# Turning softmax weights with VectorE block transposes and a round trip through DRAM instead of TensorE transposes

## The chip, the core and the metric

The kernel runs on one core of a Trainium2 chip. A core has five instruction streams that each run in order: TensorE (PE, matrix products, with its weight loads shown apart as PEld), VectorE (DVE), ScalarE (ACT), GpSimd (POOL) and SyncE (SP), which here issues nearly all DMA transfers. The metric is the device time of one execution in microseconds (us). Before the change it is 1191.92 us, the median of three runs (1191.44 to 1193.4).

## The reference, cut to what matters

Four transformer layers run one after the other over 8 batch entries of 128 tokens by 256 features, all in float32. Every layer attends to the same context of 8 x 128 x 256 (`ctx`) in some way and ends in a feed-forward network of 1024 hidden units. The first two layers have 16 heads of 16 features and turn no weights in this kernel. What the change touches is the attention of the third and the fourth layer:

```python
# third layer, twice (i = 1, 2): 16 heads of K = 128 features, one learned key and value more
qh = (q_in @ wq + bq).reshape(b, q_len, H, K)
kh = concat([(kv_in @ wk + bk).reshape(b, t, H, K), bias_k])
vh = concat([(kv_in @ wv + bv).reshape(b, t, H, K), bias_v])
logits = einsum('bqhk,bthk->bhqt', qh, kh) / sqrt(K)
weights = softmax(logits)                       # over t
ctx = einsum('bhqt,bthk->bqhk', weights, vh).reshape(b, q_len, H * K)
x = res + ctx @ wo + bo

# fourth layer: self attention (w_qkv), then attention to ctx (w_q, w_kv); 16 heads of 16
scores = einsum('bhqd,bhkd->bhqk', q, k) / sqrt(16)
scores = scores * mask - 10000.0 * (1.0 - mask)
probs = softmax(scores)
out = einsum('bhqk,bhkd->bhqd', probs, v)
```

In both, the scores come out with the queries on the 128 partitions and the keys along the row, so that the softmax is taken along a row. The second product sums over the keys, and TensorE sums over partitions: so the 128 x 128 weights of every head have to be turned (keys onto the partitions) between the softmax and that product.

## The kernel before

**Tiling.** The batch is cut into four threads of two entries each (`SIZES`, class `Thread`, lines 483 to 499). A thread goes through all four layers (`blocks`, line 1434): the first two in `front` (1464), the third as two calls of `wide_attention` (1223) and an `mlp`, the fourth in `last_block` (1489) as attentions "a4" and "a5" and an `mlp`. Threads are in different layers at the same time: a thread starts its front when the thread two before it has left its own (`FRONTS`), and at most three are ahead of the end of the third layer (`WIDES`). The last thread (number 3) does its fourth layer entry by entry (`BY_BATCH`).

**Third layer.** `wide_attention` goes over four groups of four heads (`group`, 1301). A group makes keys, queries and values of both entries, and then for each entry the scores of four heads into one PSUM bank ("tl", tile `s`) and `after_scores` (1374): the maximum (`mx`), the difference into tile `t` (128 x 516: four heads of 128 keys and the learned key at the end of each head's row), the exponential in place, the row sums (`sm`), their reciprocal, and the scaling on POOL. Then four TensorE transposes (`transposes`, 1394) take `t` against the identity `ident` into another "tl" bank; `out_of` (1204) copies it to SBUF (`pt`) on ACT or DVE, whichever is asked first; four products with the values `vw` (`weighted`, 1403) follow, and the output projection. This is done 4 threads x 2 attentions x 4 groups x 2 entries = 64 times. A `t` buffer (7 of them) is free after the transposes, a `pt` buffer (`pt_wide`, 2) after `weighted`.

**Fourth layer.** `attention` calls `by_pairs` (1103). For an entry, 16 heads' scores fill four PSUM banks ("sc"); `softmax` (1128) handles one bank of four heads (index r): scores times mask (DVE), plus the mask's second term (POOL), minimum (`mn`, DVE; signs are flipped), four exponentials with their sums (ACT), reciprocal (DVE), scaling (POOL). `values` (1152) then turns the four tiles `ts[r]` one after the other by four TensorE transposes each, copies each out (`out_of`) to its part of `pts`, and runs 32 small products (`weighted`). That is 4 threads x 2 attentions x 2 entries x 4 = 64 tiles more.

**The value bias of the third layer.** The learned value is taken out of the values: `value_bias` (1361) loads 512 numbers of `L2_bv` and 512 of `L2_bias_v` to all partitions (tiles `bv`, 2 buffers, and `bb`, 1 buffer; 256 KB each), subtracts the second from the first on POOL, and does so for every group of every thread, 32 times. `learned_keys` (1215) does the like for the keys once.

**What sets the order.** All instructions are written out once by a planner (class `Plan`, 85). Each piece of work is a Python generator with an urgency (smaller is sooner); the planner keeps a clock with a modelled duration per instruction (`_weight`, 265), and whenever an engine of the model is free, it emits on that engine the ready piece with the smallest urgency. Urgencies are the table `U` (66) plus an offset per thread and stage from `LATE` (67). Every buffer is a `Slots` counter. So the order on each engine, SP's too, is fixed at build time; on the chip an instruction waits for its inputs and holds up all that is behind it on its engine. DMA transfers go through `load` and `dma` (437 to 450), which the planner holds for done when its modelled transfer is over:

```python
        plan.dma_until = max(plan.dma_until, plan.now) + kb_ * 2.75
        yield plan.dma_until - plan.now + 2300
```

When TensorE has nothing to do and the model finds its clock in danger, `idle_work` (422) emits a product of the identity with itself. Almost every instruction passes through one helper, so that the profile puts it on line 335; the tiles' names tell them apart. A float32 product is two MATMUL records in the profile, a transpose one.

Of the kernel before, what the change touches and what calls it, by code (L numbers as in the profile page):

```python
# [14 lines left out]
AF = mybir.ActivationFunctionType  # L15
ALU = mybir.AluOpType
AX = mybir.AxisListType

P = 128
# [41 lines left out]

WARM = True
FRONTS, WIDES = 2, 3
FRONT_BY_BATCH, BY_BATCH = (0,), (3,)
AHEAD = [[(1, 0), (1, 1)], [], [], []]
U = {'take': 0.75, 'taken': -1, 'norm': 1.9, 'mask': 5.29, 'k': 2.24, 'q': 0.77, 'v': 3.01, 'by key': 0.17, 'softmax': 1.71, 'weights': 1.17, 'pairs': 0.21, 'out': 0.57, 'mlp norm': -0.61, 'mlp 1': 2.92, 'mlp 2': 3.24, 'wide norm': -0.65, 'wide k': 3.4, 'wide q': 3.13, 'wide v': 6.35, 'wide s': 4.05, 'wide': 0.91, 'ahead': 3.88, 'load': -0.56, 'early': 2.38}
LATE = [(3.86, -0.62, -1, 1.19, 0.57, -0.78, 2.63, 2.91, 2.96, 4.12, 2.25, 1.84, 0.96, 5.29, 0.08, 0.08, 1.89), (2.66, 9.69, 3.46, 1.89, 2.36, 5.53, 5.25, 5.05, 6.11, 13.74, 3.59, 9.93, 12.52, 6.5, 10.81, 5.73, 5.27), (4.81, 10.83, 3.75, -1, -0.06, 1.37, 3.1, 2.75, 1.5, 1.56, 0.96, -1, -1, 8.35, 14.37, 7.29, 0.32), (1.56, 2.87, 0.11, -0.46, 1.42, 1.31, 4.51, 3.52, 0.3, -0.41, -1, 3.2, -0.53, 2.26, 3.5700000000000003, 0.86, 0.98)]


class Event:  # L70
# [194 lines left out]
def _weight(eng, name, args, kw):  # L265
# [25 lines left out]
    if eng == "DVE":  # L291
        if name == "tensor_scalar" and n == 4 and len(aps) == 2 and len(args) > 5:
            return 145, False
        if name == "reciprocal":
            return 65 + 6.25 * n, False
        if name in ("bn_stats", "bn_aggr"):
            return (330 if name == "bn_stats" else 150), False
        if n <= 8:
            return 68 + 55 * max(0, len(aps) - 2) * (name == "tensor_scalar"), on_sbuf and name != "memset"
        if name in ("tensor_scalar", "tensor_copy") and on_sbuf:  # L300
            return 75 + 0.8 * n + 55 * by_part, True
        two = name in ("tensor_tensor", "scalar_tensor_tensor") and sum(
            x.space == bass.MemoryType.SB and x.free_size() > 1 for x in aps[1:]) == 2
        return 72 + 1.03 * n + 55 * by_part, two
# [52 lines left out]
def four_blocks(ctx: ExitStack, tc: tile.TileContext, a: dict, out: bass.AP):  # L357
# [2 lines left out]
    wpool = ctx.enter_context(tc.tile_pool(name="w", bufs=1))  # L360
    act = ctx.enter_context(tc.tile_pool(name="act", bufs=1))
    ps = ctx.enter_context(tc.tile_pool(name="ps", bufs=1, space=bass.MemoryType.PSUM))
    plan = Plan()
    nc = Engines(tc.nc, plan)
    spawn = plan.spawn
# [20 lines left out]
        return t[:, : n * w].rearrange("p (a b) -> p a b", a=n)  # L386


    NT_, NHT, NXN, NAT = 7, 4, 2, 2
    t_slots, hT_slots, xn_slots, at_slots = Slots(NT_), Slots(NHT), Slots(NXN), Slots(NAT)  # L390
    pt_small, pt_wide, tm_slots = Slots(2), Slots(2), Slots(2)
    kb_slots, v_slots = Slots(20), Slots(4)
    attn_slots, x1_slots = Slots(4), Slots(4)
    row_slots, bv_slots, bb_slots, w_slots = Slots(2), Slots(2), Slots(1), Slots(NWT)

    def kb():
        return new(act, [P, 2 * P], "kb", bufs=20)
# [705 lines left out]
    def by_pairs(T, ns, scale, mask, masks, q, k, v, v_in, vb, attnT):  # L1103
# [24 lines left out]
        def softmax(s, b, r, mn, sm, ts):  # L1128
            s = s.rearrange("p (h k) -> p h k", h=4)
            yield (t_slots, 1)  # L1130
            t = ts[r] = new(act, [P, 516], "t", bufs=NT_)[:, :512].rearrange("p (h k) -> p h k", h=4)
            bm = b % masks

            def over_heads(i):
                return mask[:, i, bm, :].unsqueeze(1).to_broadcast([P, 4, P])
            yield op("DVE", lambda: nc.vector.tensor_tensor(t, s, over_heads(0), ALU.mult))
            plan.put(sc)
            yield op("POOL", lambda: nc.gpsimd.tensor_tensor(t, t, over_heads(1), ALU.add))
            yield op("DVE", lambda: nc.vector.tensor_reduce(mn[:, r].unsqueeze(2), t, AX.X, ALU.min))

            def exps():
                for j in range(4):
                    nc.scalar.activation(
                        t[:, j, :], t[:, j, :], AF.Exp, bias=mn[:, r, j : j + 1], scale=-1.0,
                        accum_out=sm[:, r, j],
                    )
            yield op("ACT", exps, None, EXP)
            yield op("DVE", lambda: nc.vector.reciprocal(sm[:, r], sm[:, r]))
            yield op("POOL", lambda: nc.gpsimd.tensor_tensor(
                t, t, sm[:, r].to_broadcast([P, 4, P]), ALU.mult))  # L1150

        def values(b, soft, ts, turn, next_turn):
            yield turn
            pts, evs = None, []
            for r in range(4):
                yield soft[r]
                if r == 0:
                    yield (pt_small, 1)
                    pts = new(act, [P, 4, 4, P], "pt4", bufs=2)
                yield (tl, 1)  # L1160
                pt = parts(bank("tl"), 4, P)

                def transposes():
                    for i in range(4):
                        nc.tensor.transpose(
                            pt[:, i, :], ts[r].rearrange("p h k -> p (h k)")[:, i * P : (i + 1) * P], ident
                        )
                yield op("PE", transposes, 0)
                plan.put(t_slots)
                evs.append(spawn(out_of(pt, pts[:, r]), U["weights"] + late, Plan.SEEN["PE"]))  # L1170
# [6 lines left out]
            def weighted():  # L1177
                for i, (c, e) in enumerate(heads):
                    for r in range(4):
                        nc.tensor.matmul(  # L1180
                            av[32 * r : 32 * r + 32, c, :],
                            lhsT=v[:, 0, b, 4 * c + r, 16 * e : 16 * e + 32],
                            rhs=pts[:, r, i, :], start=(e == 0), stop=(e == 1),
                        )
            yield op("PE", weighted)
            plan.put(pt_small)
# [24 lines left out]

    kbs = {}
    kbs_in = Event()

    def learned_keys():
        yield cols_in
        for i in (1, 2):
            kbs[i] = new(const, [P, 16], f"kb{i}")
            yield op("POOL", lambda: nc.gpsimd.tensor_tensor(
                kbs[i], col(f"L2_bk{i}", 0, 16), col(f"L2_bias_k{i}", 0, 16), ALU.subtract))  # L1220
        plan.set(kbs_in)

    def wide_attention(T, i):
        hT, hT_in = yield from normed(
# [136 lines left out]
    def value_bias(to, i, hg, step_back):  # L1361
# [1 line left out]
        yield (bv_slots, 1)  # L1363
        bv = new(wpool, [P, 512], "bv", bufs=2)
        to.append(bv)
        e = spawn(load(bv, a[f"L2_bv{i}"][:, s].partition_broadcast(P), 256), U["load"] + step_back)
        yield (bb_slots, 1)
        bb = new(wpool, [P, 512], "bb", bufs=1)
        yield spawn(load(bb, a[f"L2_bias_v{i}"][:, s].partition_broadcast(P), 256), U["load"] + step_back)
        yield e  # L1370
        yield op("POOL", lambda: nc.gpsimd.tensor_tensor(bv, bv, bb, ALU.subtract))
        plan.put(bb_slots)

    def after_scores(T, i, hg, b, s, vs, v_in, n, v_slots):
        t = new(act, [P, 516], "t", bufs=NT_).rearrange("p (h k) -> p h k", h=4)
        mx = new(act, [P, 4, 1], "mx", bufs=4)
        sm = new(act, [P, 4, 1], "sm2", bufs=4)
        yield op("DVE", lambda: nc.vector.tensor_reduce(mx, s, AX.X, ALU.max))
        yield op("DVE", lambda: nc.vector.tensor_scalar(t[:, :, P : P + 1], mx, 0.0, -1.0, ALU.max, ALU.mult))
        yield op("DVE", lambda: nc.vector.tensor_tensor(  # L1380
            t[:, :, 0:P], s, t[:, :, P : P + 1].to_broadcast([P, 4, P]), ALU.add))
        plan.put(tl)
        yield op("ACT", lambda: nc.scalar.activation(t, t, AF.Exp), None, EXP)
        yield op("DVE", lambda: nc.vector.tensor_reduce(sm, t, AX.X, ALU.add))
        yield op("DVE", lambda: nc.vector.reciprocal(sm, sm))
        yield op("POOL", lambda: nc.gpsimd.tensor_tensor(
            t[:, :, 0:P], t[:, :, 0:P], sm.to_broadcast([P, 4, P]), ALU.mult))
        yield v_in
        yield (pt_wide, 1)
        yield (tl, 1)  # L1390
        pt = parts(bank("tl"), 4, P)
        dst = new(act, [P, 4, P], "pt", bufs=2)

        def transposes():
            for j in range(4):
                nc.tensor.transpose(pt[:, j, :], t[:, j, 0:P], ident)
        yield op("PE", transposes)
        plan.put(t_slots)
        yield from out_of(pt, dst)
        yield (tl, 1)  # L1400
        av = parts(bank("tl"), 4, P)

        def weighted():
            for j in range(4):
                nc.tensor.matmul(
                    av[:, j, :], lhsT=vs[b][:, j * P : (j + 1) * P], rhs=dst[:, j, :], start=True, stop=True)
        yield op("PE", weighted)
        plan.put(pt_wide)
        plan.put(v_slots)
# [112 lines left out]
    plan.idle_work = idle_work if WARM else None  # L1522
    spawn(inputs(), 0)
    spawn(learned_keys(), 5.0)
    plan.run()


# [40 lines left out]
```

## Time and profile before

| | |
|---|---|
| runs | 1191.44, 1191.92, 1193.4 us (median 1191.92) |
| profiled execution: span from the first to the last instruction | 1188.3 us |
| PE busy | 1151.0 us |
| DVE, ACT, POOL busy | 747.5, 595.0, 345.3 us |
| DMA | 146.61 MB, 39.3% of the engines' span in the main queue |
| transposes of the weights | 512, in quartets of one tile `t` |
| granted TensorE clock | 0.997 |

The profile is of one execution. The page gives no other time of it than its span; the median of the timed runs is 3.6 us longer. Busy time of an engine is the union of its instructions. In the groups of instructions, `out<-in` are tile names without numbers, then the shapes, then busy time, mean ns of one, and the idle time of the engine just before. A matmul's mean duration (some 275 ns for the smallest) is its passage through the pipeline; several overlap, so the time that one takes from TensorE is read from the starts in the timeline. The DMA list gives the size of a transfer and the median time from issue to landing.

### The profile page before, as it was taken

How to read it: one execution, taken by the hardware profiler on the slowest of the kernel's cores; microseconds unless marked ns; L12 is line 12 of the kernel's file. 1: busy time of each engine (PE TensorE's matmuls, PEld its weight loads, DVE VectorE, ACT ScalarE, POOL GpSimd, SP SyncE). 2: the span in 40 equal slices, each digit the busy share in tenths (PEclk: the TensorE clock that was granted, in tenths of full speed). 3: DMA queues.
4: the chain of work that ended last, by engine and by line, in shares of the span. 5: the costliest groups of instructions: out<-in, count | busy, mean ns of one | idle time of the engine just before them, and what ended most of it. 6: DMA issues, size and time to landing. Idle time of an engine off the chain costs nothing.

```text
span 1188.3 us, 22557 instructions
## 1 busy us (share of the span) xinstructions
PE 1151.0 (97%) x8518; PEld 949.1 (80%) x8518; DVE 747.5 (63%) x2021; ACT 595.0 (50%) x1519; POOL 345.3 (29%) x416
## 2 busy tenths in 40 slices
PE   8998998999999999999999999999999999999998
PEld 7687777888878788787878888887878887787776
DVE  6877578565374657767588643645443568666763
ACT  3545344344344535638346644333334357668783
POOL 3121102113021112126315311112111158545751
PEclk9999999999999999999999999999999999999999
DMA  8443241445523345362324535354544634232301
GB/s 264 144 132 99 73 112 59 139 123 160 168 85 100 125 142 165 99 193 91 116 76 133 157 133 164 101 154 130 159 148 150 177 111 126 94 103 67 99 1 63
DMA packets 109564, 146.61 MB, mean 123 GB/s; under 512 B 7440, under 2 KB 68496, under 8 KB 109456
## 3 DMA queue, kind: packets, MB, share of 16 engines
q1 hardware_dynamic: 108080, 143.99, 39.3%
q8 instruction: 68, 1.11, 0.4%
q10 hardware_dynamic: 1376, 1.18, 0.3%
q14 instruction: 40, 0.33, 0.1%
HBM read 144.09 MB, written 1.05 MB: 122 GB/s over the span
## 4 chain that ended last, share of the span: by engine, by line
PE 84%; DVE 8%; ACT 4%; DMA 2%; issue 1%; POOL 1%; ACTq 0%; SPq 0%; DVEq 0%; POOLq 0%
PE mm L335 61%; PE tl L335 18%; PE sc L335 5%; ACT t L335 1%; ACT pt L335 1%; DVE mn L335 1%; DVE t L335 1%; DVE tm L335 1%; DVE q L335 1%; DVE k L335 1%; DVE mp L335 1%; DMA ctxT<-in_ctxT 1%; ACT L335 1%; DMA w<-in_L_wk 1%; DMA bv<-in_L_bv 1%
## 5 line engine op out<-in xcount | busy, mean ns | idle before, releaser
L335 PE MATMUL mm<-hT,w 128*128 128x256 f32 (+1 forms) x1360 | 291.0, 361 | 8.8 <-issue 2.0
L335 PEld LDWEIGHTS mm<-hT,w 128*128 128x128 f32 x1360 | 231.9, 190 | 44.9 <-issue 6.1
L335 POOL TENSOR_TENSOR t<-t,sm 128x512 f32<-128x512 f32 x128 | 131.8, 1040 | 296.6 <-DVE sm L335 218.6
L335 PE MATMUL mm<-ctxT,w 128*128 128x256 f32 (+1 forms) x632 | 146.0, 376 | 5.0 <-DMA ctxT<-in_ctxT 1.7
L335 PE MATMUL mm<-w,ctxT 128*128 128x512 f32 (+1 forms) x352 | 144.1, 537 | 0.8 <-DVE k L335 0.8
L335 PEld LDWEIGHTS mm<-ctxT,w 128*128 128x128 f32 x632 | 114.6, 192 | 24.0 <-issue 6.8
L335 PE MATMUL mm<-w,at 128*128 128x256 f32 x512 | 121.5, 381 | 0.0
L335 POOL TENSOR_TENSOR x<-x,row 128x512 f32<-128x512 f32 (+1 forms) x42 | 47.1, 1121 | 254.4 <-ACT xn L335 158.3
L335 PE MATMUL mm<-w,kb 128*128 128x256 f32 x512 | 117.6, 380 | 1.7 <-issue 1.6
L335 DVE TENSOR_TENSOR x<-mm,x 128x256 f32<-128x256 f32 (+1 forms) x98 | 47.1, 481 | 114.0 <-PE mm L335 113.4
L335 PEld LDWEIGHTS mm<-w,at 128*128 128x128 f32 x512 | 94.5, 190 | 17.0 <-issue 3.4
L335 PEld LDWEIGHTS mm<-w,kb 128*128 128x128 f32 x512 | 95.2, 190 | 14.5 <-issue 2.2
L335 ACT ACTIVATE t<-t,mn 128x128 f32<-128x128 f32 x256 | 99.2, 391 | 8.5 <-DVE mn L335 6.5
L335 POOL TENSOR_TENSOR t<-t,mask 128x512 f32<-128x512 f32 x64 | 80.5, 1276 | 56.0 <-DVE t L335 51.2
L335 PEld LDWEIGHTS mm<-w,ctxT 128*128 128x128 f32 x352 | 62.4, 190 | 37.1 <-issue 31.4
L335 ACT ACTIVATE at<-tl,cols 128x128 f32<-128x128 f32 x212 | 60.4, 368 | 50.0 <-PE tl L335 46.8
L335 ACT ACTIVATE kb<-mm,cols 128x256 f32<-128x256 f32 (+1 forms) x152 | 57.0, 438 | 53.7 <-PE mm L335 53.3
L335 DVE TENSOR_SCALAR kb<-mm,cols 128x256 f32<-128x256 f32 x63 | 30.0, 483 | 80.5 <-ACT kb L335 76.7
L335 PE MATMUL tl<-ident,t 128*128 128x128 f32 x512 | 75.8, 275 | 3.9 <-ACT pt L335 1.6
L335 PEld LDWEIGHTS tl<-ident,t 128*128 128x128 f32 x512 | 60.5, 141 | 20.9 <-issue 8.2
L335 ACT ACTIVATE kb<-mm,kb 128x256 f32<-128x256 f32 x77 | 34.6, 471 | 84.7 <-PE mm L335 81.3
L335 ACT COPY pt<-tl 128x512 f32<-128x512 f32 x84 | 48.4, 584 | 56.6 <-PE tl L335 56.3
(124 smaller groups left out, 1853.5 us busy)
## 6 DMA issues: line engine op xcount, KB each, us to landing
w<-in_L_wk SPq DMA_DIRECT2D x32, 512.0 KB, 4.4
w<-in_L_wv SPq DMA_DIRECT2D x32, 512.0 KB, 3.9
w<-in_L_wq SPq DMA_DIRECT2D x32, 512.0 KB, 3.8
w<-in_L_wo SPq DMA_DIRECT2D x32, 512.0 KB, 3.9
bv<-in_L_bv SPq DMA_DIRECT2D x32, 256.0 KB, 4.8
bb<-in_L_bias_v SPq DMA_DIRECT2D x32, 256.0 KB, 5.7
w<-in_L_mlp_w SPq DMA_DIRECT2D x16, 512.0 KB, 4.4
w<-in_L_w_fc SPq DMA_DIRECT2D x16, 512.0 KB, 3.9
```

Source lines behind the costliest of these rows:

```text
L335: return f(*args, **kw)
```

## The change

`turned` is a new way to turn a tile `t` of 128 queries by four heads of 128 keys. The softmax writes `t` in another order of its row: key block j (32 keys), head h, key c in the block. DVE then transposes every 32 x 32 block in place (one instruction for the 128 x 512 tile). After it, partition 32i + c, column (j, h, a) holds the weight of query 32i + a and key 32j + c. Four DMAs (one for each i, 64 KB) write the blocks to a DRAM tile `d` with the key 32j + c as row, in runs of 512 bytes, and one DMA (256 KB) reads `d` back with the keys on the partitions. The products take the four heads out of the row by a strided access (four runs of 32).

It is used for the third layer in all threads (64 tiles) and for the fourth layer in threads 0 to 2 (`TURNED`; 48 tiles). The 16 tiles of thread 3's fourth layer are turned by TensorE as before. `t` is given free after the four stores; `pt_wide` has 3 buffers for 2; up to 8 DRAM tiles are in use. The learned key's column sits now at the end of the tile, so the sum of a row is a reduction over 128 x 4 x 4 x 32 and a small addition (`inverse`).

`learned_values` takes the difference of the two biases of the values once, on 32 partitions, and writes it to a DRAM tile `dv`; `value_bias` only loads 512 numbers of `dv` to all partitions. The tile `bb`, its 32 loads and the 32 POOL subtractions are gone. `U` and `LATE`, so the order of all work, have new values, and `U` a new entry `turn` for the five DMAs of a tile.

```diff
 FRONTS, WIDES = 2, 3
+TURNED = (0, 1, 2)
-U = {'take': 0.75, 'taken': -1, 'norm': 1.9, 'mask': 5.29, 'k': 2.24, 'q': 0.77, 'v': 3.01, 'by key': 0.17, 'softmax': 1.71, 'weights': 1.17, 'pairs': 0.21, 'out': 0.57, 'mlp norm': -0.61, 'mlp 1': 2.92, 'mlp 2': 3.24, 'wide norm': -0.65, 'wide k': 3.4, 'wide q': 3.13, 'wide v': 6.35, 'wide s': 4.05, 'wide': 0.91, 'ahead': 3.88, 'load': -0.56, 'early': 2.38}
+U = {'take': -0.02, 'taken': -5.79, 'norm': 1.94, 'mask': 3.68, 'k': 2.16, 'q': 0.51, 'v': 2.68, 'by key': -0.18, 'softmax': 8.13, 'weights': 0.55, 'pairs': 0.21, 'out': 0.7, 'mlp norm': -0.61, 'mlp 1': 2.92, 'mlp 2': 3.48, 'wide norm': -0.65, 'wide k': 3.43, 'wide q': 1.33, 'wide v': 6.42, 'wide s': 3.99, 'wide': 3.83, 'ahead': 3.34, 'load': -0.56, 'turn': -0.58, 'early': 3.32}
...
+        if name == "transpose":
+            return 75 + 1.04 * n, False
...
-    NT_, NHT, NXN, NAT = 7, 4, 2, 2
+    NT_, NHT, NXN, NAT, NPT, ND = 7, 4, 2, 2, 3, 8
...
         def softmax(s, b, r, mn, sm, ts):
             s = s.rearrange("p (h k) -> p h k", h=4)
             yield (t_slots, 1)
+            ts[r] = new(act, [P, 516], "t", bufs=NT_)[:, :512]
+            if T.h in TURNED:
+                t = ts[r].rearrange("p (j h c) -> p h j c", h=4, c=32)
+                s = s.rearrange("p h (j c) -> p h j c", c=32)
+                keys = AX.XY
...
         def values(b, soft, ts, turn, next_turn):
...
+                if T.h in TURNED:
+                    evs.append(spawn(turned(ts[r], t_slots, None, pts[:, r]), U["weights"] + late))
+                    continue
...
-                            rhs=pts[:, r, i, :], start=(e == 0), stop=(e == 1),
+                            rhs=of_head[:, r, i], start=(e == 0), stop=(e == 1),
...
+    def learned_values():
+        of = new(const, [32, 2, P], "dv")
+        ends = [spawn(load(of[16 * (i - 1) : 16 * i, k], a[f"L2_{n}{i}"].rearrange("o (h d) -> (o h) d", d=P), 8), U["load"] - 1)
+                for i in (1, 2) for k, n in enumerate(("bv", "bias_v"))]
+        for e in ends:
+            yield e
+        yield op("POOL", lambda: nc.gpsimd.tensor_tensor(of[:, 0], of[:, 0], of[:, 1], ALU.subtract))
+        yield spawn(load(dv.rearrange("(h d) -> h d", d=P), of[:, 0], 16), U["load"] - 1)
+        plan.set(dv_in)
...
-        e = spawn(load(bv, a[f"L2_bv{i}"][:, s].partition_broadcast(P), 256), U["load"] + step_back)
-        yield (bb_slots, 1)
-        bb = new(wpool, [P, 512], "bb", bufs=1)
-        yield spawn(load(bb, a[f"L2_bias_v{i}"][:, s].partition_broadcast(P), 256), U["load"] + step_back)
-        yield e
-        yield op("POOL", lambda: nc.gpsimd.tensor_tensor(bv, bv, bb, ALU.subtract))
-        plan.put(bb_slots)
+        yield dv_in
+        yield spawn(load(bv, dv[2048 * (i - 1) :][s].unsqueeze(0).partition_broadcast(P), 256), U["load"] + step_back)
+
+    def turned(t, t_slots, slots, made):
+        yield op("DVE", lambda: nc.vector.transpose(t, t))
+        yield (d_slots, 1)
+        d = new(dram, [P, 512], "d", bufs=ND)
+        to = d.rearrange("(j r) (i x) -> r i j x", j=4, i=4)
+        ends = []
+        for i in range(4):
+            ends.append(spawn(load(to[:, i], t[32 * i : 32 * i + 32].rearrange("r (j x) -> r j x", j=4), 64), U["turn"]))
+        for e in ends:
+            yield e
+        plan.put(t_slots)
+        if slots:
+            yield (slots, 1)
+        dst = made() if slots else made
+        yield spawn(load(dst.rearrange("p i h c -> p (i h c)"), d, 256), U["turn"])
+        plan.put(d_slots)
+        return dst
 
     def after_scores(T, i, hg, b, s, vs, v_in, n, v_slots):
...
-        yield op("DVE", lambda: nc.vector.tensor_reduce(sm, t, AX.X, ALU.add))
-        yield op("DVE", lambda: nc.vector.reciprocal(sm, sm))
...
+        def inverse():
+            nc.vector.tensor_reduce(sm, by_head, AX.XY, ALU.add)
+            nc.vector.tensor_tensor(sm, sm, rest, ALU.add)
+            nc.vector.reciprocal(sm, sm)
+        yield op("DVE", inverse)
+        yield op("POOL", lambda: nc.gpsimd.tensor_tensor(by_head, by_head, over_keys(sm), ALU.mult))
+        dst = yield from turned(blocks_, t_slots, pt_wide, lambda: new(act, [P, 4, 4, 32], "pt", bufs=NPT))
         yield v_in
-        yield (pt_wide, 1)
-        yield (tl, 1)
-        pt = parts(bank("tl"), 4, P)
-        dst = new(act, [P, 4, P], "pt", bufs=2)
-
-        def transposes():
-            for j in range(4):
-                nc.tensor.transpose(pt[:, j, :], t[:, j, 0:P], ident)
-        yield op("PE", transposes)
-        plan.put(t_slots)
-        yield from out_of(pt, dst)
...
-                    av[:, j, :], lhsT=vs[b][:, j * P : (j + 1) * P], rhs=dst[:, j, :], start=True, stop=True)
+                    av[:, j, :], lhsT=vs[b][:, j * P : (j + 1) * P], rhs=dst[:, :, j, :], start=True, stop=True)
...
+    spawn(learned_values(), 5.0)
```

## Prediction

> **What bounds the kernel now.** I read the busy times first, then the windows by stage, then the chain of work that ended last, and then the rows that price the parts.
>
> ```profile
> PE 1151.0 (97%) x8518; PEld 949.1 (80%) x8518; DVE 747.5 (63%) x2021; ACT 595.0 (50%) x1519; POOL 345.3 (29%) x416
> PE 84%; DVE 8%; ACT 4%; DMA 2%; issue 1%; POOL 1%; ACTq 0%; SPq 0%; DVEq 0%; POOLq 0%
> ```
>
> TensorE is busy 97% of the span and holds 84% of the chain. The windows (length; busy time and count of PE, PEld, DVE, ACT, POOL; clock; DMA share; GB/s) say where:
>
> ```profile
> 200.00:1000.00 800.00, 796.19 (x5282) 657.05 (x5281) 475.68 (x1203) 370.95 (x915) 204.23 (x227) 1.00 0.43 133
> 929.00:1103.00 174.00, 170.25 (x1283) 141.02 (x1285) 123.22 (x339) 116.50 (x386) 96.95 (x101) 1.00 0.35 109
> 1120.00:1140.00 20.00, 17.27 (x157) 14.24 (x156) 17.06 (x60) 13.88 (x44) 13.23 (x18) 1.00 0.04 11
> ```
>
> From 200 to 1000 us TensorE idles 3.8 us in 800: what is taken off its queue there shortens the run, if nothing else becomes late. From 929 to 1103 us (fourth layer of threads 1 and 2 beside the third layer of thread 3) it is still busy 170.25 of 174 us, but DVE already 71%. At the end it is no longer the bound: at 1120 to 1140 us DVE is busy 85%, PE 86%.
>
> The rows that price the change (the groups; two stretches of TensorE's timeline with start and length; DMA issues with median landing time; the main DMA queue with packets, MB and share; waits with total, times and longest; two pieces of the chain):
>
> ```profile
> L335 PE MATMUL tl<-ident,t 128*128 128x128 f32 x512 | 75.8, 275 | 3.9 <-ACT pt L335 1.6
> 718.52 0.60 PE L335 MATMUL tl<-ident,t 128*128 128x128 f32 x4
> 718.96 3.40 PE L335 MATMUL mm<-ctxT,w 128*128 128x256 f32 x15
> ...
> 1024.56 0.66 PE L335 MATMUL tl<-ident,t 128*128 128x128 f32 x4
> 1025.14 1.08 PE L335 MATMUL tl<-pt,v 128*32 128x128 f32 x32
> ...
> L335 ACT COPY pt<-tl 128x512 f32<-128x512 f32 x84 | 48.4, 584 | 56.6 <-PE tl L335 56.3
> L335 DVE COPY pt<-tl 128x512 f32<-128x512 f32 x44 | 29.7, 683 | 5.9 <-PE tl L335 5.7
> L335 DVE STREAM_SHUFFLE tm<-tm 128x256 f32<-128x256 f32 x8 | 3.5, 437 | 0.0
> L335 POOL TENSOR_TENSOR bv<-bv,bb 128x512 f32<-128x512 f32 x32 | 40.8, 1274 | 111.0 <-DMA bb<-in_L_bias_v 97.8 <-DVE pt L335 6.2 <-DVE mv L335 4.3
> ...
> bv<-in_L_bv SPq DMA_DIRECT2D x32, 256.0 KB, 4.8
> w<-in_L_w_q SPq DMA_DIRECT2D x4, 256.0 KB, 2.8
> mask<-in_mask_s SPq DMA_DIRECT2D x5, 64.0 KB, 4.0
> out<-x SPq DMA_DIRECT2D x2, 128.0 KB, 1.8
> q1 hardware_dynamic: 108080, 143.99, 39.3%
> PE tl L335 <- ACT pt L335: 5.8, 10, 1.4
> SPq L335 <- PE mm L335: 710.9, 177, 18.1
> 804.67 6.31 DMA bv<-in_L_bv
> 813.82 6.34 DMA w<-in_L_wk
> ```
>
> A quartet of transposes, from its start to the start of what follows, takes 0.44 us ahead of a projection and 0.58 ahead of the small products. The last two lines show SP's queue holding work up: the load of `bb` stood on SP until POOL had done with the one buffer, and the weight load behind it left late; TensorE then waited 1.4 us for those weights.
>
> **The change part by part.** *Transposes off TensorE.* 64 tiles of the third and 48 of the fourth layer make 112 quartets. After 1103 us the trace has 84 transposes, 21 quartets; 16 are thread 3's and stay, so 5 of the removed ones lie where TensorE is no bound. 107 x 0.44 = 47.1 us; with 0.58, 62 us. I take 47.1, since most quartets stand among projections. Their copies (112 of 128) free ACT of some 74 x 0.584 = 43 us and DVE of 38 x 0.683 = 26 us, off the path.
>
> *Block transposes on DVE.* No such row. The nearest are the 128x512 copy (0.683 us) and the shuffle (0.294 us for 128 columns, 0.437 for 256, so 0.72 for 512). I take 0.69: 112 x 0.69 = 77 us. `inverse` adds a small addition, 64 x 0.17 (the reciprocal's row) = 11 us. DVE goes from 747 to about 747 + 77 - 26 + 11 = 809 us, 70% of the new span. It is covered where PE is full, but not evenly: from 929 to 1103 us the trace has 140 transposes, 35 quartets, all turned now. There DVE gets 123.2 + 35 x 0.69 - 10 copies x 0.68 + 8 x 0.17 = 142 us of the 174 - 15 = 159 left: 89%. Bounds for what that costs TensorE: nothing (DVE still has 17 us of room), or what the stretch 1120 to 1140 us shows at 85% DVE, 14% of idle PE, 22 us less the 3.8 idle now = 18. I take 7: other threads' work stands ready here, as it does not in that stretch.
>
> The Trainium skill (VectorE: DVE Perf Modes, Rules for kernel authors) advises the opposite of this change: TensorE for a 128 x 128 transpose if the result may lie in PSUM. Its section on the three transpose paths gives 390 ns for TensorE and 311 ns for VectorE's blocks in bf16. By these 448 transposes would free 175 us of TensorE, where the trace's spacing of 110 ns gives 49.
>
> *The detour.* Per tile on SP: four stores of 64 KB and one load of 256 KB, 560 in all, less the 32 of `bb`. An issue takes 0.37 to 0.45 us in SP's rows, so 560 x 0.4 = 224 us more on a queue that now issues some 395 transfers (158 us): a third of the span. Latency of one tile: 0.69 on DVE, 1.6 for four issues, 1.8 to 4.0 for the last store to land (the 128 KB store at the end; the 64 KB loads under traffic), 0.4, and 2.8 to 4.8 for the load: 7.3 to 11.5 us, say 9. Now it is 1.5 us (at 718.52 the quartet starts, at 720.03 its copy is over). 7.5 us more per tile are hidden as long as TensorE has other ready work ahead of the tile's products in its order. Behind a waiting store or load on SP stand weight loads and other tiles' transfers; behind a late load stands `weighted`, and behind that all of TensorE. Bounds for the 76 such products (64, and 12 entries of the fourth layer): nothing, as the loads of before show (3.1 us of TensorE's waits on DMA in the whole run); or 1.4 us each, the wait above, 106 us. For 200 to 929 us I take nothing: a group of the third layer keeps TensorE some 17 us (keys, queries, values and output projection at 3.46 us per 16 records of the chain, and four times 0.9 for scores and `weighted`), so there are 17 us of work for every two detours of 9. The end of an attention of the third layer has no such cover inside its thread: the next norm waits for its last tile. For thread 3, twice 7.5 = 15 us, or nothing while threads 1 and 2 fill in; PE's 98% from 929 to 1103 speaks for the low end; I take 4.
>
> The Trainium skill (DMA: Bandwidth & Descriptors, Rules for kernel authors) says that transfers under 64 KB pay mostly overhead and wants small ones merged; its fit for GpSimd's transfers (Anatomy of one DMA), 2.0 us plus bytes/436e3, would make a store 2.15 us and a load 2.6, an estimate below most of the rows above, and the detour 7.4 us, 5.9 more than now.
>
> *DMA load.* 112 x 512 KB, less 32 x 256 KB, is 50 MB more on 144. By bytes the queue's share goes to 53%; by packets (448 x 128 of 512 B, 112 x 128 of 2 KB, less 32 x 128, at the present 69 ns each) to 64%. Weights then land later than 4 us; what covers it is that a thread holds four weight buffers. Price 0; without cover it is in the 106 us above.
>
> *Value bias.* POOL is freed of 40.8 us that nobody waited for; SP no longer stands behind `bb`. I take back the 1.4 us at 820 us and 0.5 around it: 1.9. At the start `bv` now waits for `learned_values`: four loads (7.5 us by the slowest start row), a subtraction under 1.3, a store of 4.0 and a load of 8.1 after 17 us end at 38 us; the first use is at 48.5 us. Price 0, up to 3 if late.
>
> *Strided products.* Runs of 32 in the moving operand: no row. On DVE the copy into `v` with holes takes 424 ns, the plain one 416. Price 0; a quarter more on 64 x 0.9 and 12 x 1.0 us would be 17 us.
>
> *New urgencies.* They move everything. The 19 us that TensorE idles in the first 200 us may shrink or grow; 0, between -8 and +10.
>
> *Sum.* 1188.3 - 47.1 - 1.9 + 7 + 4 = 1150.3 us of span. The runs' median lies 3.6 above the span: 1154 us.
>
> **The rivals.** *The gain is eaten late, still faster.* DVE binds from 929 us on (+18) and thread 3's hand-offs are bare (+15): 1188.3 - 47.1 - 1.9 + 33 + 3.6 = 1176; between 1172 and 1189. For it: 89% on DVE. Against: PE's ready work there.
>
> *Slower: TensorE waits at `weighted` for the detour's load.* Place: the load of `d` behind other transfers on SP, as at 804 to 820 us, where two transfers of 6.3 us stood one behind the other. Decides from 47/76 = 0.6 us per product on. At half of the 76 paying 1.4 us the gain is about gone; at all, 1188.3 - 49 + 106 + 3.6 = 1249. For it: SP takes waits in order, and its longest wait for a weight buffer is 18.1 us. Against: those waits are SP's spare time, and TensorE's hand-overs from the copies (`PE tl` on `ACT pt`), just as tight in the order, cost it 5.8 us in all.
>
> *No change:* both effects cancel, 1190 to 1194.
>
> **How the numbers follow.** Likeliest 0.55, its own range 1132 to 1172 (the larger quartet and a lucky order at one end, the taken costs doubled at the other). Late loss 0.23. No change 0.03. Slower 0.19. A difference of 0.2% (2.4 us) is about what a measurement of this kernel can tell from none. Faster 0.78, same 0.03, slower 0.19. Range: from 1130 (quartets at 0.58, no costs: 1188.3 - 62 - 1.9 + 3.6 = 1128) to 1200, which takes in the late loss and the cheapest of the slower case.
>
> **What would show it.** `ident,t` falls from 512 to 64 and PE's busy time to about 1101 us plus any idle products. DVE shows 112 transposes near 0.69 us; stores land within 4 us, the load of `d` within 5. TensorE's waits for DMA of `pt` stay under 10 us; idle PE from 929 us on grows by about 10. Wrong: PE waits on `pt` of tens of us, block transposes well over 0.7 us, weights landing late, or idle PE spread over the middle.

## Result: 0.9% slower

The changed kernel takes 1201.16 us (median; 1200.28 to 1206.38) against 1192.1 us (with one more run of the kernel before); the ratio is 1.0094, 95% interval 1.0069 to 1.0119. The profiled execution has a span of 1198.5 us and took 1200.28 us, so what lies around a span is 1.8 us here. The forecast was 1154, in a range of 1130 to 1200.

The profile after, first the busy times and the shares of the chain that ended last, then two windows (length; busy time and count of PE, PEld, DVE, ACT, POOL; clock; DMA share; GB/s):

```profile
PE 1126.3 (94%) x8134; PEld 915.2 (76%) x8134; DVE 803.4 (67%) x2156; ACT 551.6 (46%) x1431; POOL 306.7 (26%) x387
PE 66%; DMA 12%; DVE 12%; ACT 5%; SPq 2%; issue 2%; POOL 1%; ACTq 0%; DVEq 0%; POOLq 0%
...
200.00:1000.00 800.00, 774.93 (x4983) 629.20 (x4983) 525.69 (x1337) 334.95 (x841) 173.92 (x205) 1.00 0.60 178
929.00:1103.00 174.00, 154.23 (x1095) 122.88 (x1094) 135.13 (x346) 92.66 (x337) 87.85 (x90) 0.96 0.70 200
```

TensorE's busy time fell by only 24.7 us, and its idle time went from 37.3 to 72.2 us. From 200 to 1000 us, where it idled 3.8 us before, it now idles 25. In the late window it is busy 154 us of 174 (before 170), and its granted clock is 0.96, where it was 1.00 before. In the chain, DMA has gone from 2% to 12% and TensorE from 84% to 66%: the run is no longer one queue.

The groups that answer to the prices, then transfers, waits and the weights' landing times (of the change, and in the last line of the kernel before):

```profile
L338 DVE STREAM_TRANSPOSE t<-t 128x512 f32<-128x512 f32 x112 | 78.1, 700 | 10.9 <-POOL t L338 10.7
L338 PE MATMUL tl<-pt,vw 128*128 128x128 f32 x512 | 68.1, 277 | 6.7 <-DMA pt<-d 5.1 <-PE mm L338 0.6 <-PE tl L338 0.5
L338 PE MATMUL mm<-ident 128*128 128x128 f32 x134 | 27.8, 328 | 4.7 <-ACT kb L338 2.0 <-POOL ident masks.py:199 1.4
L338 PE MATMUL tl<-ident 128*128 128x128 f32 x56 | 10.4, 301 | 0.5
...
d<-t SPq DMA_DIRECT2D x448, 64.0 KB, 2.2
pt<-d SPq DMA_DIRECT2D x112, 256.0 KB, 3.5
q1 hardware_dynamic: 184288, 194.41, 55.1%
...
PE tl L338 <- DMA pt<-d: 7.5, 6, 2.5
PE sc L338 <- DVE q L338: 6.6, 1, 6.6
SPq L338 <- DMA d<-t: 31.8, 32, 3.7
...
DMA to landing us min/median/max: 2.5/4.9/11.1
...
DMA to landing us min/median/max: 2.5/4.0/9.4
```

The block transposes and the transfers take about as long as the rows of before said. TensorE waits for the turned tile itself only 7.5 us. The rest of its idle time is spread over more than twenty kinds of waits of a few us. The products of the identity with itself, which fill holes in the planned order, are 190 records and 38.2 us (126 and 23.6 before). The last two lines are those of the weight tiles `w`: median 4.9 us from issue to landing, before 4.0.

The longest of the waits, 6.6 us for `q`, shows how it happens. The chain of the changed kernel from 998 to 1028 us (start, length, what):

```profile
998.62 6.67 DMA pt<-d
...
1006.68 5.88 DMA w<-in_L_wq
...
1012.70 1.98 PE mm L338 x8
...
1016.64 0.62 SPq L338
...
1017.30 9.08 DMA mask<-in_mask_x
...
1026.41 0.59 DVE mask L338
1027.00 0.47 DVE q L338
```

Twelve stores, four loads of turned tiles and some weights had been issued in the 13 us before the fourth layer's mask (128 KB, median landing 4.0 us before). The mask landed after 9.08 us. A DVE instruction on it stood before the one that makes `q`, and TensorE stood still until `q` was there. Two windows show the DMA engines while the mask was under way, and the clock while TensorE stood still and went on:

```profile
1010.00:1024.00 14.00, 10.43 (x87) 8.67 (x85) 6.56 (x20) 4.76 (x10) 2.04 (x2) 1.00 0.84 254
1024.00:1034.00 10.00, 5.71 (x35) 4.23 (x36) 6.55 (x13) 1.20 (x2) 4.75 (x4) 0.50 0.75 213
```

The DMA engines were busy 84% of the first stretch, and TensorE's clock was at half in the second. That second stretch is most of what makes the clock 0.96 in the late window.

### The profile page after: what moved, and what is told of

Read it like the earlier page. It is cut to its first block, busy times and chain, and to the rows that moved or that the text cites. A ratio compares the mean times of both kernels' runs of the same rounds, so it can differ in the third digit from the quotient of the medians.

```text
span 1198.5 us, 22971 instructions
## 1 busy us (share of the span) xinstructions
PE 1126.3 (94%) x8134; PEld 915.2 (76%) x8134; DVE 803.4 (67%) x2156; ACT 551.6 (46%) x1431; POOL 306.7 (26%) x387
## 3 DMA queue, kind: packets, MB, share of 16 engines
q1 hardware_dynamic: 184288, 194.41, 55.1%
## 4 chain that ended last, share of the span: by engine, by line
PE 66%; DMA 12%; DVE 12%; ACT 5%; SPq 2%; issue 2%; POOL 1%; ACTq 0%; DVEq 0%; POOLq 0%
PE mm L338 51%; PE tl L338 11%; PE sc L338 4%; SPq L338 2%; DMA w<-in_L_wq 2%; DVE t L338 2%; DMA w<-in_L_wk 1%; DMA pt<-d 1%; DVE tm L338 1%; DVE mp L338 1%; DVE rz L338 1%; ACT t L338 1%; ACT kb L338 1%; ACT q L338 1%; ACT L338 1%
## 5 line engine op out<-in xcount | busy, mean ns | idle before, releaser
L338 PEld LDWEIGHTS mm<-hT,w 128*128 128x128 f32 x1360 | 234.8, 193 | 58.6 <-issue 5.7
L338 ACT ACTIVATE at<-tl,cols 128x128 f32<-128x128 f32 x192 | 54.6, 368 | 72.1 <-PE tl L338 47.6
L338 ACT ACTIVATE kb<-mm,sb 128x256 f32<-128x256 f32 x75 | 33.6, 471 | 114.2 <-PE mm L338 111.9
L338 DVE STREAM_TRANSPOSE t<-t 128x512 f32<-128x512 f32 x112 | 78.1, 700 | 10.9 <-POOL t L338 10.7
L338 PEld LDWEIGHTS tl<-pt,vw 128*128 128x128 f32 x512 | 65.3, 191 | 17.0 <-issue 6.2
L338 PE MATMUL tl<-pt,vw 128*128 128x128 f32 x512 | 68.1, 277 | 6.7 <-DMA pt<-d 5.1
```

The costliest lines, as they stand in the source:

```text
L338: return f(*args, **kw)
```

## Experiments

All of them but e8, e12 and e15 keep the planner's order of one of the two kernels instruction by instruction: what is left out is still charged on the planner's clock, so that the run differs by the missing work alone. Differences between runs are taken from their ratios to the kernel before (times 1190 us); an interval of a ratio is some ±0.2% (±0.4% in e5).

**e1, only the gain.** The quartets and copies of the 112 tiles are left out of the kernel before.

```diff
-        yield op("PE", transposes)
+        yield left_out("PE", 4 * 109)
         plan.put(t_slots)
-        yield from out_of(pt, dst)
+        yield from out_of(None, None)
...
-                    av[:, j, :], lhsT=..., rhs=dst[:, j, :], start=True, stop=True)
+                    av[:, j, :], lhsT=..., rhs=even_w[:, j, :], start=True, stop=True)
```

> The kernel before, in its own order, with the 112 quartets of transposes and their copies left out and nothing in their place (the weighted products of these tiles read ctxT instead of the turned weights, so the output is another). It measures the first term of the sum alone. If TensorE's queue is the bound wherever I said, 47 us come off: 1192 - 47 = 1145, between 1130 and 1150. The rival, that the quartets stand in gaps that other work sets, leaves less than half: above 1168.

1158.7 us, ratio 0.9742 (0.9723 to 0.9761): 30.7 us faster. Busy times and the window of 200 to 1000 us of this run:

```profile
PE 1102.6 (95%) x8070; PEld 900.8 (78%) x8070; DVE 725.4 (63%) x1982; ACT 556.9 (48%) x1446; POOL 345.4 (30%) x416
200.00:1000.00 800.00, 786.19 (x5094) 641.23 (x5095) 477.43 (x1226) 356.64 (x916) 222.65 (x246) 1.00 0.45 137
```

TensorE's busy time fell by 48.4 us, as the quartets' spacing says. But 15 us of it came back as idle time, 10 of them between 200 and 1000 us, where it had been busy 99.5%. There it now waits for what DVE and ACT make, above all for `q` (3.6 us in 4 waits), `vw` (2.8 in 3) and `attnT` (2.0 in one). A queue that is never empty in the profile doesn't say how late the next thing would be if the queue were shorter. So in this order even a free way of turning would have given 31 us and not 47.

**e2 to e4, taking the detour away in the order of the change.** e2: the products read `ctxT`, so that TensorE never waits for a turned tile; everything else is done. e3: the 560 transfers are left out too. e4: the block transposes as well.

```diff
# e2
-rhs=dst[:, :, j, :]
+rhs=even_w[:, :, j, :]          # a view of ctxT
# e3, besides
-load(to[:, i], t[32 * i : 32 * i + 32]..., 64)
+no_load(64)
-load(dst.rearrange("p i h c -> p (i h c)"), d, 256)
+no_load(256)
# e4, besides
-yield op("DVE", lambda: nc.vector.transpose(t, t))
+yield op("DVE", not_done)
```

> The changed kernel in its own order with all of the detour's transfers and block transposes, but the products read ctxT instead of the turned tile, so that TensorE never waits for the detour itself (the output is another). Theory A (TensorE waits at the products for the load of d): falls by tens of us towards 1155. Theory B (the transfers hold up others on SP and on the DMA engines, or DVE is late): stays within 12 us of 1201, since the profile after shows only 7.5 us of such waits.

> As the run before, and the 560 transfers of the detour are left out too; the order of everything else is the same (the output is another). Theory B by transfers: falls to 1160 to 1175, weights land in about 4 us again and TensorE's idle time falls by 20 us or more. Theory C (the order that the new urgencies and the longer detour give is looser in itself): stays above 1190. Theory D (DVE): stays above 1190, and falls only in the next run.

> As the run before, and the 112 block transposes on DVE are left out as well (78 us of DVE). Theory D (DVE's load holds TensorE up): 10 us or more below the run before. If the transfers alone are to blame: within 5 us of the run before. If the order itself is to blame, this one too stays above 1185, although nothing of the detour is left.

| | median us | ratio to before | interval |
|---|---|---|---|
| the change | 1201.16 | 1.0094 | 1.0069 to 1.0119 |
| e2, no wait for the tile | 1202.1 | 1.0110 | 1.0092 to 1.0128 |
| e3, no transfers either | 1181.63 | 0.9939 | 0.9919 to 0.9959 |
| e4, no block transposes either | 1172.87 | 0.9863 | 0.9843 to 0.9883 |
| e1, bare, in the order of before | 1158.7 | 0.9742 | 0.9723 to 0.9761 |

The direct wait is worth nothing (theory A falls). The transfers cost 20.4 us, the block transposes 9.0, and 14.4 us are left between e4 and e1, which both have nothing in place of the quartets. Those two differ in the order, and besides in small parts of the change that e4 still has: the value bias taken once, the addition in `inverse`, the strided reads and the third `pt` buffer. The rows of e4:

```profile
PE 1116.2 (95%) x8134; PEld 911.2 (78%) x8134; DVE 739.9 (63%) x2044; ACT 550.6 (47%) x1431; POOL 306.7 (26%) x387
L338 PE MATMUL mm<-ident 128*128 128x128 f32 x134 | 27.5, 334 | 4.7 <-ACT kb L338 1.7 <-POOL ident masks.py:199 1.4 <-DVE x L338 0.7
```

TensorE idles nearly as long as in e1 (54.7 and 52.3 us), but is busy 13.6 us longer, which is the additional products of the identity with itself (37.8 us with their second group, against 23.8). The planner put them where its model had no ready work for TensorE. So all of theories B, C and D hold a part.

**e5 and e6, what about the transfers.** In e5 the load of a tile reads an input instead of `d`, so SP doesn't wait for the stores. In e6 every store carries 16 KB for 64 and every load 16 for 256; issues and waits remain.

```diff
# e5
-load(dst.rearrange("p i h c -> p (i h c)"), d, 256)
+load(dst.rearrange("p i h c -> p (i h c)"), a["L0_fc_w"][:P, :512], 256)
# e6
-load(to[:, i], t[32 * i : 32 * i + 32].rearrange("r (j x) -> r j x", j=4), 64)
+load(to[:, i, 0], t[32 * i : 32 * i + 32, :P], 64)
-load(dst.rearrange("p i h c -> p (i h c)"), d, 256)
+load(dst.rearrange("p i h c -> p (i h c)")[:32, :P], d[:32, :P], 256)
```

> The changed kernel in its own order; the 256 KB load of each tile reads 128 rows of an input instead of the tile's own DRAM buffer, so that it does not wait on SP for the four stores (the output is another). All transfers are still made. If SP's waits for the stores (31.8 us in 32 waits in the profile after) hold up what stands behind them: falls by 8 us or more, below 1193. If the transfers' traffic or their mere issue is the cost: stays within 4 us of 1201.

> The changed kernel in its own order with all 560 transfers, their issues and their waits on SP, but each store carries 16 KB instead of 64 and each load 16 KB instead of 256; the products read ctxT (the output is another). If traffic on the DMA engines (weights landing 0.9 us later at the median) is what the 20 us of the run without transfers are: falls to 1182 to 1188. If SP's order and issue time are: stays at 1195 or more. Between, both.

e5: 1205.01 us, ratio 1.0122 (1.0086 to 1.0158): without SP's waits for the stores nothing is gained. e6: 1187.56 us, 0.9976 (0.9960 to 0.9992). The products read `ctxT` here as in e2. Against e2, which differs from it in the bytes (and packets) alone, that is 16 us; against e3, 4.4 us are left for 560 issues and their waits on SP. So most of the cost goes with the bytes. That does not clear SP's queue, since short transfers also shorten what stands on it; e10 shows a place where both met.

**e7, the detour's transfers on ACT's queue.**

```diff
+    def load_on_act(dst, src, kb_):
+        def f(eng):
+            plan.weight += 480
+            tc.nc.scalar.dma_start(out=dst, in_=src)
+        return dma(f, kb_, False)
```

> The changed kernel, correct output, same order; the detour's 560 transfers are issued on ACT's queue in the same places instead of SP's. If SP's head-of-line waits and the shared queue are the main cost: 1185 to 1193. Against it stands that ACT, busy 552 us, gets 560 issues of some 0.4 us, 224 us, and their waits for DVE and for the stores: if that weighs more, above 1201.

1274.59 us, 1.0692 (1.0657 to 1.0727): far worse. From its waits (total, times, longest):

```profile
ACT kb L338 <- DMA d<-t: 38.1, 10, 12.1
PE mm L338 <- ACT kb L338: 21.5, 14, 3.8
```

ACT now stands still until the stores have landed before it can issue a load, and all that it should copy out of PSUM stands behind that; TensorE waits for those copies. SP, which computes nothing, is the better place here.

**e8 and e12, the two tables exchanged.** e8 is the changed kernel with the old `U` and `LATE` (and 'turn': -0.58), e12 the kernel before with the new ones.

```diff
# e8
-U = {..., 'softmax': 8.13, ...}    # and LATE
+U = {..., 'softmax': 1.71, ... 'turn': -0.58, ...}
```

> The changed kernel with the urgencies of before (U and LATE; 'turn' at -0.58 as in the change). In the run without transfers and blocks the new order was 14 us slower than the bare old one. If the new urgencies are that loss: about 1187. If the old urgencies suit the longer way of the weights worse, as the new ones were chosen for it: above 1205.

> The kernel before with the urgencies of the change (correct output). If the new urgencies were better or neutral in themselves: 1192 or less. If each table fits only the work it was chosen for, as the changed kernel with the old table suggests (1216): above 1205.

e8: 1216.39 us, 1.0212 (1.0182 to 1.0243). e12: 1240.06 us, 1.0421 (1.0405 to 1.0437). Each table fits its own work only. The new table is worth 14 us (1.2%) to the change, and the 14.4 us of e4 against e1 are therefore not a badly chosen table that the old one would mend. How much of them is the longer way that the planner had to plan around, how much an imperfect table and how much the small parts that e4 keeps isn't separated by these runs.

**e9, the value bias alone**, in the order of before: its difference is taken once (four small loads on ACT's queue at the start, a subtraction, a store ahead of the first `bv`), `bb` and the 32 subtractions are left out in their places.

```diff
-        bb = new(wpool, [P, 512], "bb", bufs=1)
-        yield spawn(load(bb, a[f"L2_bias_v{i}"][:, s].partition_broadcast(P), 256), U["load"] + step_back)
+        yield spawn(dma(no_load, 256, False), U["load"] + step_back)
...
-        yield op("POOL", lambda: nc.gpsimd.tensor_tensor(bv, bv, bb, ALU.subtract))
+        yield op("POOL", no_subtraction)
```

> The kernel before in its own order, with one part of the change alone: the difference of the two value biases is taken once and stored to DRAM, each bv load reads it, and the 32 loads of bb and the 32 subtractions on POOL are left out in their places (correct output). My prediction took 1.9 us for this: 1190, within 0.3% of before. If SP's hold-up behind bb were worth more than the one wait on the chain: 1187 or less, which would beat both kernels. If the store and its receipt at the start cost: up to 1194.

1188.8 us, 0.9988 (0.9974 to 1.0002): 1.4 us, not told apart from nothing.

**e10, no transfers for the fourth layer's 48 tiles.**

```diff
+        return load(dst, src, kb_) if third_layer else dma(f, kb_, False)    # f issues nothing
```

> The changed kernel in its own order; the transfers of the 48 tiles of the fourth layer are left out and their products read ctxT (the output is another), those of the 64 tiles of the third layer are kept. All transfers together cost 20 us. If they hurt where they crowd, in the late stretch with the fourth layer of two threads: most of it comes back, below 1187. If they hurt by number, evenly: 48 of 112, so 9 us, about 1192.

1185.66 us, 0.9960 (0.9946 to 0.9975). Against the change that is 16 us of 20 for 48 tiles of 112. The window of 1000 to 1100 us, of the change and of this run:

```profile
1000.00:1100.00 100.00, 85.13 (x641) 67.62 (x640) 75.01 (x198) 54.56 (x196) 47.29 (x50) 0.95 0.73 210
```

```profile
1000.00:1100.00 100.00, 91.69 (x708) 74.21 (x707) 80.84 (x226) 60.42 (x200) 50.84 (x55) 0.97 0.36 110
```

The transfers hurt where they crowd: with the fourth layer's, the DMA engines are busy 73% in this stretch and TensorE 85%; without them 36% and 92%. Where the time is lost can be read more closely, since TensorE runs the same 8134 records in the same order in both traces. The change is 4.6 us behind this run at the last record before the wait for `q`, 11.4 us at the first one after it, 14.2 at 1050 us and 14.0 at the end. So some 10 of the 14 us lie around one wait. The mask's issue on SP and TensorE's records there, first in the change, then in this run:

```profile
1017.30 0.68 SPq L338 DMA_DIRECT2D mask<-in_mask_x  x1
1027.51 1.99 PE L338 MATMUL sc<-k,q 32*128 32x128 f32 x24 [6.61 <-DVE q L338]
...
998.14 0.43 SPq L338 DMA_DIRECT2D mask<-in_mask_x  x1
1015.78 1.17 PE L338 MATMUL sc<-k,q 32*128 32x128 f32 x32
```

The mask leaves 19.2 us earlier here, of which TensorE's own lead explains about 4, and lands after 4.5 us, 11 us before DVE takes it up. In the change it stood on SP behind the stores and loads of turned tiles and then landed 4.6 us more slowly: the queue and the traffic together used up its lead.

**e11, no block transposes, all transfers.**

```diff
-yield op("DVE", lambda: nc.vector.transpose(t, t))
+yield op("DVE", not_done)
```

> The changed kernel in its own order with all transfers, without the 112 block transposes on DVE (the output is another). If DVE's and the transfers' costs are separate and add up: 1201 - 9 = 1192, as between the two runs without transfers. If the transfers alone set what is late: within 3 us of 1201.

1189.47 us, 0.9988 (0.9974 to 1.0002): 12.6 us below the change, against 9.0 in the pair without transfers. The two costs add up, within the intervals.

**e13 and e14, the products of the identity with itself.** They are left out after 200 us of the planner's clock, in e13 in the change (54 of them), in e14 in the kernel before together with e9's edit (24).

```diff
+                if plan.now > 200000:
+                    plan.weight += 225
+                    return True
                 nc.tensor.matmul(bank(tag)[:, :P], lhsT=ident, rhs=ident, start=True, stop=True)
```

> The changed kernel, correct output, same order, without the 54 products of the identity with itself that the planner placed after 200 us of its clock. If they are a cost in themselves: 1201 - 54 x 0.22 = 1189. If they fill time in which the next product isn't ready anyway: within 4 us of 1201. If the clock falls without them: slower.

> The kernel before in its own order with the value bias taken once (as in e9) and without the 24 products of the identity with itself after 200 us of the planner's clock (correct output). If such products are a cost in themselves: 1190 - 1.3 - 24 x 0.22 = 1183.5, faster than both kernels. If they fill idle time: 1189.

e13: 1204.18 us, 1.0107 (1.0085 to 1.0130); e14: 1189.26 us, 0.9991 (0.9975 to 1.0008), the same as e9. Leaving the products out gains nothing in either kernel, so they fill time that would be idle. The granted clock is lower without them (0.979 in e13 and 0.990 in the change; 0.993 in e14 and 0.999 in e9), so a small cost and a small benefit that cancel are not excluded. I read the 14 us of e4 against e1 as TensorE without ready work, which the profile shows as such products more than as idle time; no run leaves the products out of e4 itself.

**e15, only the third layer through DRAM.**

```diff
-TURNED = (0, 1, 2)
+TURNED = ()
```

> The changed kernel with only the third layer turned through DRAM (TURNED empty, the planner makes its own order with the new urgencies; correct output). By the parts measured: 64 of 112 quartets gain 18, their transfers cost 5, their blocks 5, and an order with tables not chosen for it costs 15 or more: 1195 to 1215. If the fourth layer's crowd alone is what makes the change lose: below 1190.

1213.03 us, 1.0197 (1.0180 to 1.0215), in an order that the planner made with a table not chosen for it. It says nothing of what a table of its own would give. No kernel tried here that does the whole work is faster than the one before beyond its interval.

## Why the prediction was wrong, by its own steps

Measured terms, each a difference of two runs (with the same order in all but the second): -30.7 (quartets, e1) + 14.4 (the order with the small parts of the change, e4 against e1) + 9.0 (block transposes, e3 against e4) + 20.4 (transfers, e2 against e3) - 1.9 (the wait for the tile, within the intervals) = +11.2 us. The forecast's terms were -47.1, -1.9, +7 and +4.

- **Transposes off TensorE** (47.1 us of gain): the size of the busy time was right (48.4 us in e1), the step from busy time to span was not. "What is taken off its queue there shortens the run, if nothing else becomes late": something did, for 15 us. The term measured 30.7.
- **Block transposes on DVE**: 0.69 us taken, 0.700 measured; 809 us of DVE forecast, 803.4 measured. Cost 7 taken between 0 and 18, 9.0 to 12.6 measured. Right in kind and place: of the 9.5 us between the traces of e3 and e4, which have the same records in the same order, 5.6 arise from 950 us on.
- **The detour's latency**: stores 2.2 us (1.8 to 4.0 taken), loads 3.5 (2.8 to 4.8); issues 0.43 and 0.38 us. TensorE's wait at the products was taken at nothing, and e2 shows that it is worth nothing.
- **DMA load, "Price 0"**: this is the step that failed most. The share of the queue was right (55.1%, between 53 and 64), and so was that weights would land later (4.9 for 4.0 us). But the cover I named, four weight buffers of a thread, covers weights in the mean. It doesn't cover the mask of the chain above, which waits its turn on SP behind the detour's transfers, nor a stretch in which the share is 73%. In its place the runs showed 20.4 us for the transfers. e6 puts 16 us on the bytes, e10 puts 16 of the transfers' 20 on the fourth layer's 48 tiles, and its trace some 10 around the one wait behind the mask. SP standing behind the detour, which the prediction names and takes at nothing, has its share in that wait; how the 20.4 us divide between queue and traffic is open. I had priced the late stretch for DVE and not for DMA, though the 27 tiles of the fourth layer that I counted there bring 14 MB in 174 us.
- **New urgencies, 0 between -8 and +10**: the term measured 14.4, if the whole of e4 against e1 is put here. The mistake was to think of them as shuffling what is there; the planner also has to place a longer way for every tile, and I take it that TensorE has less ready work in its order. The runs show the size, not this cause.
- **Value bias**: 1.9 taken; 1.4 measured, not told from nothing.
- **Strided products**: taken at 0; `tl<-pt,vw` takes 68.1 us in 512 records, before 68.0.
- **Hand-offs at thread 3's ends** (4 us) were not measured by themselves.

The slower rival had the sign but not the mechanism: I saw TensorE waiting for the load of `d` behind other transfers; what the costliest wait shows is the reverse, another transfer waiting behind the detour's. Its counter-argument, that the waits for copies cost TensorE only 5.8 us, was about the wrong hand-over. The late-loss rival named the right stage, with DVE where DMA stood.

The weighing against the Trainium skill: its advice (VectorE: DVE Perf Modes, Rules for kernel authors) to turn 128 x 128 on TensorE stood against the change, and no way through DRAM that was run here beat it. Its 390 ns per transpose, for bf16, is not what a stream of them takes here in float32, 110 ns; and the 31 us that they were really worth are about as much as the other way cost in transfers and blocks. Its rule on small transfers (DMA: Bandwidth & Descriptors, Rules for kernel authors) names overhead as the price of those under 64 KB. The detour's are of 64 and 256 KB; cut to 16 KB in e6, all 560 cost 4.4 us, and 16 us had gone with the bytes.

## What to carry to other kernels

Time taken off a full queue comes back only as far as the next engine lets it: leave the work out, with the order kept, before building something in its place (e1: two thirds came back). Moving work to an engine or to DMA queues with spare time on average is priced in the stage where it crowds, and for the transfers that stand behind the new ones on the issuing queue. Where a planner fixes the order, separate order and work by keeping the one while taking away the other; two traces with the same order can then be laid side by side, record by record, to see where the time goes. A table of urgencies tuned for one kernel cost another 1 to 4%.

## What the runs showed of the hardware that I had not expected

- A DMA issued from an engine that computes held up its computing until what the transfer waits for was there: 560 transfers moved from SP to ACT cost 71 us (ratios 1.0094 and 1.0692), although ACT was busy only 46% in the change. The longest of these waits, before a copy to `kb`, was 12.1 us.
- The 16 us that go with the bytes arise at a DMA share of 55% over the whole span, at which weights landed after 4.9 us for 4.0. Such a mean hides the crowd: 73% from 1000 to 1100 us, 84% from 1010 to 1024, when the mask took 9.08 us.
- TensorE's granted clock, 0.997 before, went to 0.990 in the change and 0.979 without the filling products (e13); in e1, with 52.3 us of idle time, it was 0.999, so the sum of idle time doesn't set it. The longest low stretch of the change is the half clock from 1024 to 1034 us, which begins while TensorE stands still for 6.6 us. What the clock cost in time isn't told apart here, since e13 and the change agree within their intervals.
